# A softmax's maxima subtracted on TensorE under a second set of scores, in a four-layer attention stack

## The chip, the cores and the metric

The kernel runs on one core of one Trainium2 chip. The metric is the device time of one execution in microseconds (us). The engines are named as in the profile: PE is TensorE's matmul, PEld its weight load, DVE VectorE, ACT ScalarE, POOL GpSimd, SP the queue that issues DMAs.

## The reference

Input x has 16 sequences of 128 tokens with 256 features; a context of the same shape is given. Four layers follow one another, each with 16 heads of 16 features and a feed-forward part:

- the first attends over the heads inside each token (16 x 16 scores per token) and has a feed-forward of 1024;
- the second has two attentions, over x itself and over the context, in which the queries, keys, values and attention weights are rounded to steps of a given size (8 bits): `_fq(x) = (clip(round(x / delta) + zp, 0, 255) - zp) * delta`, and `softmax(_fq(q) @ _fq(k).T * 0.25)` is itself rounded to 8 bits with `zp` 0 before it meets the values; then a gated feed-forward;
- the third and fourth have two plain attentions each (softmax of q k / 4, some with masks) and a feed-forward.

Every softmax takes each row's maximum away before the exponential. In the second layer the scores, before their scale, are sums of products of integers.

## The kernel before

The 16 sequences go in 8 groups of two. `group` writes each group's work as steps; a step has a price per engine that may do it, the tiles it reads and writes, and a function that issues its instructions. All groups' steps go through one planner, `Plan.order`, which places them on the engines by prices, dependencies and free slots, and a shift per group and stage (`LEADS`); `least` is the earliest due time of a step. So the order on every engine is fixed when the kernel is built, and a change of any price moves steps everywhere. Every engine works its own queue strictly in that order. Where a step offers two engines, the planner picks one.

Memory: a large arena in SBUF, four PSUM banks `pw` for products and transposes, and one PSUM slot `ps` of four banks for scores (`SLOTS`, line 67). One set of scores for one sequence and 16 heads is 128 x 2048 fp32 and fills `ps`, so only one set is in flight at a time.

The second layer's attention is `quantized_attention` (line 1046) with `attention` (line 899): 8 groups x 2 attentions x 2 sequences = 32 batches. For a batch, `begin` (1091) issues the scores: eight bf16 matmuls of 32 rows, four strips of the array at once (`scores`, 832; line 844). Then `soft` does each half (8 heads, 128 x 1024) by itself: DVE takes the negated row maxima (1100), DVE adds them to the scores, out of PSUM into the arena (1113), ACT takes the exponential in place with the scale (1119), DVE sums the rows, inverts and scales the sums (1125 to 1128), POOL multiplies and rounds head by head (1134), ACT makes bf16 of it (1139). For 2 of the 64 halves the planner chose another way: ACT does eight exponentials with the maximum as bias and the row sum on the side (1104, 1106). A transposing DMA turns each half (913), and `products` (878, line 892) multiplies it with the values.

The third and fourth layers' attention is `plain_attention` (1199), 64 batches. It has the scores once in `ps` for the maxima (1243, or 1250 and 1255 under a mask), splits the negated maxima into three bf16 pieces whose sum is exact (1264 to 1272, DVE or POOL), transposes them on TensorE (1274), copies them to SBUF (1276), and then forms the scores a second time, transposed, with the maxima already added: 32 matmuls of 32 rows (1292), of which 16 are fp32 products of keys and queries and 16 are bf16 products that lay the maxima of one head over its block, with the constant 0/1 matrix `three_of` as weights. In that loop, for each of four heads of a strip, keys come first in the even ones and maxima in the odd ones. In the masked cross attention of layer three, `laid` (852, line 855) lays a mask under the scores in the same way, four bf16 matmuls of 512 columns.

Other lines that the prediction names: 686 and 699 are the fp32 products with weights (four matmuls, eight records in the trace, per step), 658 the transposes, 645 the loads of weights, 745 or 746 the addition or multiplication of a row (POOL or DVE), 732 or 733 the normalisation (ACT or DVE), 674 or 675 the scaling after a transpose, 1310 and 1313 the plain exponentials.

Of the kernel before, what the change touches and what calls it, by code (L numbers as in the profile page):

```python
# [8 lines left out]
F32 = mybir.dt.float32  # L9
BF16 = mybir.dt.bfloat16  # L10
I32 = mybir.dt.int32
U8 = mybir.dt.uint8
AF = mybir.ActivationFunctionType
ALU = mybir.AluOpType
AX = mybir.AxisListType

P = 128
B, S, D, H, DH, FF = 16, 128, 256, 16, 16, 1024
# [54 lines left out]


LEADS = [
    [79, -243, 396, 61, 306, 431, -218, 552, 246, -1043, 475, -1, 382, -725, -212, 120, 529, 352, 259, 257],
    [-1469, -506, -432, -870, -252, -175, -212, -889, -146, -178, -511, -754, -160, -374, -1202, -416, -1438, 67, -497, -72],
    [-408, -392, -516, 558, -136, 688, -438, -458, -1053, 58, -79, 304, 253, -385, -261, -277, -707, 386, 101, -525],
    [-618, -910, 247, -450, -186, 137, 135, 293, -265, -318, 61, -448, 441, -1039, -573, 1607, 326, 1399, 704, 1265],
    [118, 30, 704, -227, 45, 608, 400, 898, 1076, 334, 689, -396, 866, 605, -189, 715, 221, 931, 98, 676],  # L80
    [136, -318, -131, -829, 314, 611, -344, 561, 524, -90, 424, -258, 680, 156, 257, 416, 338, 931, 1112, 654],
    [117, 16, 354, -72, -34, 620, 249, 955, -58, -43, -427, 64, 340, 435, 246, 1312, 557, 1079, 605, 296],
    [586, 96, 831, 335, 623, 330, -23, 781, 930, 238, 205, 94, 1033, -120, -401, 948, 200, 1214, 848, 332],
]
CONTEXT = 18
HANDOVER = {"PE": 0.25, "-": 0.0}
# [65 lines left out]
class Plan:  # L152
# [3 lines left out]
    def block(self, kind, shape, dtype=F32, role=None):  # L156
        b = Block(kind, shape, dtype)
        if role is not None:
            sec = self.section
            b.section, b.role, b.turn = sec, role, sec.made[role]  # L160
            sec.made[role] += 1
            sec.units[role] = max(sec.units[role], b.units)
        return b
# [264 lines left out]
def decoder_stack_kernel(ctx: ExitStack, tc: tile.TileContext, a: dict, out: bass.AP):  # L428
# [97 lines left out]
    def small(n, *shape):  # L526
        return block("sm", [P, n] if not shape else [P, *shape])
# [4 lines left out]
    def prepare():  # L532
# [33 lines left out]

            G.tensor_scalar(m1, m1, -1.0e9, 1.0, ALU.mult, ALU.mult)

        step([("POOL", 5.0, masks)], reads=[raw, dl_token], writes=[mask_token], least=110.0)


        for dst, n, src, eye, dtype in ((m1T, S, m1, ident, F32), (kmT, B, km, ident[:B, :B], F32), (m3T, S, m3, ident, F32)):
# [287 lines left out]
    def paired(e):  # L860

        return e.rearrange("p (s i) k -> p s i k", i=2) if len(e.shape) == 3 else e.rearrange("p (s i) -> p s i", i=2)

    def wide(v):
        return paired(v).unsqueeze(3).to_broadcast([P, 4, 2, S])

    def values(dtype):


# [29 lines left out]
    def attention(x, wo, begin, soft, out_of, vz, dtype, after):  # L899


        plan.enter(after=after, w=1, oT=1, e=2, eT=2, **({"r": 1} if dtype == F32 else {"eb": 2}))
        wo = weight(wo)
        oT = block("m", [P, 2, NT], role="oT")
        for j in range(GB):
            ps, held = begin(j)
            eTs = []
            for c in range(2):
                e = soft(ps, j, c, held[c])
                eT = block("m", [P, 8, S], dtype, role="eT")  # L910
                eTs.append(eT)
                step(
                    [("SP", 1.2, lambda e=e, eT=eT: nc.sync.dma_start_transpose(out=eT.ap(), in_=e.ap().rearrange("p q k -> p (q k)")), None, 1.0)],
                    reads=[e], writes=[eT],
                )
            out_of(oT, eTs, vz, j)
        ps = psum()
        tokens_first(wo, oT, ps)
        add_to(x, ps)
# [126 lines left out]
    def quantized_attention(x, i, hT, kvT):  # L1046
# [44 lines left out]
        def begin(j):  # L1091
            tok = slice(j * S, (j + 1) * S)
            ps, issue = scores(None, lambda r, c: qT(r, c, tok), lambda r, c: kz(r, c, tok), True)
            es = [block("m", [P, 8, S], role="e") for _ in range(2)]
            step([("PE", 0.24, issue, "rows")], reads=[qk], writes=[ps], holds=es[:1])
            return ps, es

        def soft(ps, j, c, e):
            m, r, bias = small(8), small(8), small(8)
            step([("DVE", 1.22, lambda: V.tensor_reduce(paired(m.ap()), ps.ap()[:, :, c], AX.X, ALU.max, negate=True))], reads=[ps], writes=[m])  # L1100
            along = lambda: taken.eng == "ACT"

            def per_head():
                A.activation(bias.ap(), m.ap(), AF.Copy, scale=one(sc))
                for q in range(8):
                    A.activation(
                        e.ap()[:, q, :], ps.ap()[:, q // 2, c, q % 2], AF.Exp, bias=bias.ap()[:, q : q + 1], scale=one(sc),
                        accum_out=r.ap()[:, q : q + 1],
                    )

            taken = step(
                [
                    ("DVE", 1.22, lambda: V.tensor_tensor(paired(e.ap()), ps.ap()[:, :, c], wide(m.ap()), ALU.add), None, 2.6),  # L1113
                    ("ACT", 6.0, per_head, "exp"),
                ],
                reads=[ps, m], writes=[e, r, bias],
            )
            step(
                [("ACT", lambda: 0.0 if along() else 1.3, lambda: None if along() else A.activation(e.ap(), e.ap(), AF.Exp, scale=one(sc)), "exp")],  # L1119
                reads=[e], writes=[e],  # L1120
            )

            def inverse():
                if not along():
                    V.tensor_reduce(r.ap(), e.ap(), AX.X, ALU.add)  # L1125
                V.reciprocal(r.ap(), r.ap())

                V.tensor_scalar(r.ap(), r.ap(), delta(3), 0.0, ALU.mult, ALU.max)  # L1128

            step([("DVE", lambda: 0.5 if along() else 1.72, inverse)], reads=[e], writes=[r])  # L1130

            def share():
                for q in range(8):
                    G.tensor_scalar(e.ap()[:, q, :], e.ap()[:, q, :], r.ap()[:, q : q + 1], MAGIC, ALU.mult, ALU.add)  # L1134

            step([("POOL", 3.15, share)], reads=[e, r], writes=[e])
            eb = block("m", [P, 8, S], BF16, role="eb")

            step([("ACT", 1.05, lambda: A.activation(eb.ap(), e.ap(), AF.Relu, bias=top, scale=-1.0))], reads=[e], writes=[eb])  # L1139
            return eb  # L1140
# [4 lines left out]
            step([("ACT", 0.48, lambda: A.activation(oT.ap()[:, :, j * S : (j + 1) * S], po.ap(), AF.Copy, scale=one(dwv)))], reads=[po], writes=[(oT, j)])  # L1145

        attention(x, wo, begin, soft, out_of, vz, BF16, [*qk.writer.values()])

    def keys_and_values(kvT, wk, wv, biases, kz, vz):
        pk, pv = psum(), psum()  # L1150
# [48 lines left out]
    def plain_attention(x, qxT, kvT, ws, biases, mask=None, masked=None, cost=0.9, masked_T=None, key_mask=None, held=(), may_be_empty=False, there=None):  # L1199
# [29 lines left out]
        def batch(j):  # L1229
# [29 lines left out]
                if may_be_empty:  # L1259
                    step([("DVE", 0.18, with_key)], reads=[m], writes=[m])  # L1260

            def split(eng, m=m, rest=rest, mq=mq):
                piece = lambda n: mq.ap().rearrange("p (s r) -> p s r", r=32)[:, :, 0:12].rearrange("p s (f n) -> p s f n", n=3)[:, :, :, n]
                four = lambda t: t.ap().rearrange("p (s f) -> p s f", f=4)
                eng.tensor_copy(piece(0), four(m))  # L1267
                eng.tensor_tensor(four(rest), four(m), piece(0), ALU.subtract)
                eng.tensor_copy(piece(1), four(rest))
                eng.tensor_tensor(piece(2), four(rest), piece(1), ALU.subtract)  # L1270

            step([("DVE", 1.0, lambda split=split: split(V)), ("POOL", 1.25, lambda split=split: split(G))], reads=[m], writes=[rest, mq])
            pt, mt = block("pw", [P, S], BF16), block("m", [P, S], BF16, role="mt")
            step([("PE", 0.1, lambda pt=pt, mq=mq: T.transpose(pt.ap(), mq.ap(), ident_b))], reads=[mq], writes=[pt], holds=[mt])
            step(
                [("ACT", 0.32, lambda pt=pt, mt=mt: A.copy(mt.ap(), pt.ap())), ("DVE", 0.25, lambda pt=pt, mt=mt: V.tensor_copy(mt.ap(), pt.ap()))],
                reads=[pt], writes=[mt],
            )

            eTs = [block("m", [P, 8, S], role="eT") for _ in range(2)]  # L1280

# [2 lines left out]
            def issue(pT=pT, mt=mt, tok=tok):  # L1284
                if masked_T is not None:
                    laid(pT.ap(), *masked_T)
                for f in range(4):
                    c, i = divmod(f, 2)
                    for part in (0, 1) if i else (1, 0):
                        for s in range(4):  # L1290
                            r = strip(s)
                            T.matmul(  # L1292
                                pT.ap()[:, s, c, i], lhsT=kz.ap()[r, c, i, tok] if part else three_of[r, f, :],
                                rhs=qT.ap()[r, c, tok] if part else mt.ap()[r],
                                start=masked_T is None and part == 1 - i, stop=(f == 3 or masked_T is None) and part == i,
                            )

            step(
# [181 lines left out]
```

## Time and profile before

| what | value |
|---|---|
| median of 3 runs | 1440.99 us |
| lowest, highest | 1439.8, 1448.02 us |
| profiled execution, its own time | 1440.68 us |
| its span, first to last instruction | 1438.9 us |
| mean granted TensorE clock | 0.98 |

A group's row in the profile reads: line, engine, operation, out<-in by tile name, shapes, count | busy time, mean ns of one | idle time of the engine just before, and what ended it. A timeline row reads: start us, length us, engine, line, operation, tiles, shape, count. The matmul records of four strips overlap, so the time that a group costs TensorE is read from its start to the next group's start. The slices are 40 equal parts of the span, about 36 us each.

### The profile page before, as it was taken

What the parts mean: (1) busy time and instruction counts of PE and PEld (TensorE: products, weight loads), DVE (VectorE), ACT (ScalarE), POOL (GpSimd) and SP (SyncE); (2) the same over time, 40 slices, a digit from 0 to 9 for tenths busy, and PEclk for the clock granted to TensorE, in tenths of its full rate; (3) what the DMA queues carried; (4) which work ended last, traced back from release to release, by engine and by line L of the source; (5) the groups of instructions that cost most, each with busy time, mean ns of one, the idle gap of its engine ahead of it and who ended that gap; (6) DMA issues with size and microseconds to landing.
All of it is one profiled execution on the core that took longest, in us unless ns stands there. A gap on an engine that the chain in (4) does not pass through costs nothing.

```text
span 1438.9 us, 36661 instructions
## 1 busy us (share of the span) xinstructions
PE 1358.0 (94%) x15219; PEld 1116.4 (78%) x15219; DVE 1042.8 (72%) x1608; ACT 837.6 (58%) x1480; POOL 596.8 (41%) x1393
## 2 busy tenths in 40 slices
PE   8899969986989999898998999999999999999998
PEld 7778857875868888687786888888887887878887
DVE  1663597888897578959788777867786867685961
ACT  4662568876675766646547656646553545366442
POOL 2022575847777236615515453434122425141201
PEclk9999989998999999999999999999999999999999
DMA  7466434442432326422221431200022111000000
GB/s 231 104 187 203 167 81 126 129 110 56 111 74 58 90 50 176 115 90 77 74 68 45 108 96 28 89 16 17 2 92 71 39 64 31 32 2 2 9 17 22
DMA packets 192646, 113.67 MB, mean 79 GB/s; under 512 B 139088, under 2 KB 181728, under 8 KB 192352
## 3 DMA queue, kind: packets, MB, share of 16 engines
q1 hardware_dynamic: 192480, 111.33, 28.3%
q8 instruction: 119, 1.95, 0.5%
q14 instruction: 47, 0.39, 0.1%
HBM read 67.26 MB, written 27.26 MB: 66 GB/s over the span
## 4 chain that ended last, share of the span: by engine, by line
PE 79%; DVE 9%; ACT 2%; issue 1%; POOL 1%; DMA 1%; SPq 0%; DVEq 0%; ACTq 0%; POOLq 0%
PE pw L699 27%; PE pw L686 27%; PE pw L892 9%; PE ps L1292 6%; PE ps L844 5%; PE pw L658 3%; DVE arena L1113 2%; DVE sm L1100 2%; DVE sm L1125 1%; DVE arena L962 1%; DVE sm L1243 1%; PE pw L987 1%; DVE arena L1250 1%; DVE sm L1255 1%; DVE sm L715 0%
## 5 line engine op out<-in xcount | busy, mean ns | idle before, releaser
L686 PE MATMUL pw<-arena 128*128 128x256 f32 x2048 | 486.9, 388 | 10.6 <-ACT arena L674 8.2
L699 PE MATMUL pw<-arena 128*128 128x256 f32 x2048 | 481.1, 386 | 2.1 <-ACT arena L665 1.6
L686 PEld LDWEIGHTS pw<-arena 128*128 128x128 f32 x2048 | 383.3, 193 | 80.4 <-issue 11.3
L699 PEld LDWEIGHTS pw<-arena 128*128 128x128 f32 x2048 | 382.6, 192 | 64.1 <-issue 9.2
L1134 POOL TENSOR_SCALAR arena<-arena,sm 128x128 f32<-128x128 f32 x512 | 186.7, 386 | 106.1 <-DVE sm L1128 71.9
L1325 DVE RECIPROCAL arena<-pw 128x256 f32<-128x256 f32 x64 | 112.1, 1752 | 90.1 <-PE pw L892 77.2
L745 POOL TENSOR_TENSOR arena<-arena,rows 128x512 f32<-128x512 f32 x109 | 139.4, 1281 | 84.7 <-ACT arena L732 72.2
L812 ACT ACTIVATE arena<-pw,cols_sb 128x256 f32<-128x256 f32 x188 | 80.0, 471 | 77.7 <-PE pw L686 70.9
L707 DVE TENSOR_TENSOR arena<-pw,arena 128x512 f32<-128x512 f32 x88 | 59.9, 682 | 77.4 <-PE pw L699 76.9
L732 ACT ACTIVATE arena<-arena,sm,sm 128x256 f32<-128x256 f32 x151 | 83.8, 595 | 31.8 <-POOL sm L725 30.7
L1292 PE MATMUL ps<-arena 32*128 32x128 f32 x2048 | 97.4, 299 | 3.3 <-DVE sm L1243 2.5
L1139 ACT ACTIVATE arena<-arena,top 128x1024 bf16<-128x1024 f32 x64 | 73.4, 1147 | 41.4 <-POOL arena L1134 35.5
L892 PE MATMUL pw<-arena 128*32 128x128 f32 (+1 forms) x2560 | 88.5, 266 | 9.1 <-DMA arena<-arena 5.3
L844 PE MATMUL ps<-arena 32*128 32x256 f32 (+1 forms) x1280 | 84.7, 371 | 12.0 <-DVE arena L1113 11.4
L658 PE MATMUL pw<-ident,arena 128*128 128x128 f32 x416 | 69.0, 292 | 27.1 <-ACT arena L732 19.3
L1292 PEld LDWEIGHTS ps<-arena 32*128 32x128 f32 x2048 | 75.8, 188 | 23.0 <-issue 10.4
L721 POOL TENSOR_SCALAR sm<-sm 128x2 f32<-128x2 f32 x88 | 17.2, 195 | 183.7 <-DVE sm L716 179.5
L1267 POOL CAST mq<-sm 128x16 bf16<-128x16 f32 x50 | 11.1, 222 | 196.1 <-DVE sm L1243 107.6
L1310 ACT ACTIVATE arena<-arena 128x1024 f32<-128x1024 f32 x64 | 66.5, 1054 | 41.5 <-DVE arena L1306 40.5
L872 POOL MEMSET arena<- 128x512 f32 (+1 forms) x48 | 25.0, 526 | 155.4 <-PE pw L699 56.9
L1119 ACT ACTIVATE arena<-arena,sc 128x1024 f32<-128x1024 f32 x62 | 70.6, 1147 | 31.3 <-DVE arena L1113 31.2
L1250 DVE TENSOR_TENSOR arena<-ps,m 128x1024 f32<-128x1024 f32 x64 | 78.0, 1219 | 12.4 <-PE ps L844 8.0
(141 smaller groups left out, 2069.4 us busy)
## 6 DMA issues: line engine op xcount, KB each, us to landing
mha<-arena SPq DMA_DIRECT2D x16, 512.0 KB, 4.5
ca<-arena SPq DMA_DIRECT2D x16, 512.0 KB, 4.2
arena<-mha SPq DMA_DIRECT2D x16, 512.0 KB, 5.2
arena<-ca SPq DMA_DIRECT2D x16, 512.0 KB, 3.9
arena<-in_L_xattn_ff_w_dram SPq DMA_DIRECT2D x29, 256.0 KB, 3.0
dqkv<-arena SPq DMA_DIRECT2D x8, 768.0 KB, 4.0
arena<-dqkv SPq DMA_DIRECT2D x16, 384.0 KB, 4.0
arena<-in_L_xattn_ffn_w_dram SPq DMA_DIRECT2D x18, 256.0 KB, 3.2
```

What stands on the lines that cost most here:

```text
L658: T.transpose(p[:, c, j * S : (j + 1) * S], s[:, j, c * P : (c + 1) * P], ident)
L686: T.matmul(ps.ap()[:, m, :], lhsT=w.ap()[:, k, m * P : (m + 1) * P], rhs=t.ap()[:, k, :], start=(k == 0), stop=(k == 1),)
L699: T.matmul(ps.ap()[:, j, :], lhsT=lhs(k, j) if lhs else t.ap()[:, k, j * S : (j + 1) * S], rhs=w.ap()[:, k, :], start=start and j + k == 0 ...
L732: ("ACT", 0.6, lambda j=j: A.activation(xh.ap()[:, j, :], x.ap()[:, j, :], AF.Identity, bias=nb.ap()[:, j : j + 1], scale=rstd.ap()[:, j : ...
L745: ("POOL", 1.33, lambda: G.tensor_tensor(dst.ap(), src.ap(), row(name), op)),
L812: "ACT", 0.47, lambda ps=ps, h=h, m=m, bias=bias: A.activation(h.ap()[:, m, :], ps.ap()[:, m, :], func, bias=bias),
L844: T.matmul(ps.ap()[:, s, c] if i is None else ps.ap()[:, s, c, i], lhsT=left(r, c) if i is None else left(r, c, i), rhs=right(r, c), start ...
L892: T.matmul(po.ap()[32 * s : 32 * s + 32, 2 * ones + c, :], lhsT=lhsT, rhs=n255 if n else eTs[c].ap()[:, 2 * s + i, :], start=i == n == 0, ...
L1134: G.tensor_scalar(e.ap()[:, q, :], e.ap()[:, q, :], r.ap()[:, q : q + 1], MAGIC, ALU.mult, ALU.add)
L1250: [("DVE", 1.22, lambda e=e, c=c: V.tensor_tensor(paired(e.ap()), ps.ap()[:, :, c], mask[0].unsqueeze(1).unsqueeze(1).to_broadcast([P, 4, ...
L1292: T.matmul(pT.ap()[:, s, c, i], lhsT=kz.ap()[r, c, i, tok] if part else three_of[r, f, :], rhs=qT.ap()[r, c, tok] if part else mt.ap()[r], ...
L1325: step([("DVE", 1.75, lambda po=po, r=r: V.reciprocal(r.ap(), po.ap()[:, 2:4, :]))], reads=[po], writes=[r])
```

## The change

Four things are changed.

1. In `quantized_attention`, `begin` now issues the scores, takes all 16 heads' negated maxima in one DVE instruction, splits, transposes and copies them by the helper `turned_maxima` (taken out of `plain_attention`, unchanged), and issues the scores a second time into `ps`, under which four bf16 matmuls of 512 columns lay the maxima. `soft` takes the exponential on ACT straight out of PSUM; the subtraction on DVE and the way with eight exponentials are gone. The attention's section holds one more small tile (`mt=1`).
2. In `plain_attention`, the loop of the 32 transposed matmuls issues all 16 laid ones first and then the 16 of keys and queries.
3. The step that makes `three_of` has its due time at 75 in place of 110.
4. The table `LEADS` has other numbers, so that the order on every engine is another one.

```diff
-        plan.enter(after=after, w=1, oT=1, e=2, eT=2, ...)
+        plan.enter(after=after, w=1, oT=1, mt=1, e=2, eT=2, ...)
...
-            step([("PE", 0.24, issue, "rows")], reads=[qk], writes=[ps], holds=es[:1])
+            step([("PE", 0.24, issue, "rows")], reads=[qk], writes=[ps])
+            m, rest, mq = small(16), small(16), block("mq", [P, P], BF16)
+            step(
+                [("DVE", 2.3, lambda ps=ps: V.tensor_reduce(m.ap(), ps.ap().rearrange("p s c i k -> p (s c i) k"), AX.X, ALU.max, negate=True))],
+                reads=[ps], writes=[m],
+            )
+            mt = turned_maxima(m, rest, mq)
+
+            def less(ps):
+                for s in range(4):
+                    T.matmul(
+                        ps[:, s].rearrange("p c i k -> p (c i k)"), lhsT=mt.ap()[strip(s)],
+                        rhs=three_of[strip(s)].rearrange("p f k -> p (f k)"), start=True, stop=False,
+                    )
+
+            ps, issue = scores(less, lambda r, c: qT(r, c, tok), lambda r, c: kz(r, c, tok), True)
+            step([("PE", 0.46, issue, "rows")], reads=[qk, mt, mask_token], writes=[ps], holds=es[:1])
...
-            step([("DVE", 1.22, lambda: V.tensor_reduce(paired(m.ap()), ps.ap()[:, :, c], AX.X, ALU.max, negate=True))], reads=[ps], writes=[m])
...
-                    ("DVE", 1.22, lambda: V.tensor_tensor(paired(e.ap()), ps.ap()[:, :, c], wide(m.ap()), ALU.add), None, 2.6),
-                    ("ACT", 6.0, per_head, "exp"),
...
+                [("ACT", 1.15, lambda: A.activation(paired(e.ap()), ps.ap()[:, :, c], AF.Exp, scale=one(sc)), "exp")],
+                reads=[ps], writes=[e],
...
+    def turned_maxima(m, rest, mq):
+        def split(eng):
+            piece = lambda n: mq.ap().rearrange("p (s r) -> p s r", r=32)[:, :, 0:12].rearrange("p s (f n) -> p s f n", n=3)[:, :, :, n]
+            four = lambda t: t.ap().rearrange("p (s f) -> p s f", f=4)
+            eng.tensor_copy(piece(0), four(m))
+            eng.tensor_tensor(four(rest), four(m), piece(0), ALU.subtract)
+            eng.tensor_copy(piece(1), four(rest))
+            eng.tensor_tensor(piece(2), four(rest), piece(1), ALU.subtract)
+        step([("DVE", 1.0, lambda: split(V)), ("POOL", 1.25, lambda: split(G))], reads=[m], writes=[rest, mq])
+        pt, mt = block("pw", [P, S], BF16), block("m", [P, S], BF16, role="mt")
+        step([("PE", 0.1, lambda: T.transpose(pt.ap(), mq.ap(), ident_b))], reads=[mq], writes=[pt], holds=[mt])
+        step(
+            [("ACT", 0.32, lambda: A.copy(mt.ap(), pt.ap())), ("DVE", 0.25, lambda: V.tensor_copy(mt.ap(), pt.ap()))],
+            reads=[pt], writes=[mt],
+        )
+        return mt
...
-                for f in range(4):
-                    c, i = divmod(f, 2)
-                    for part in (0, 1) if i else (1, 0):
+                for part in range(2):
+                    for f in range(4):
+                        c, i = divmod(f, 2)
                         for s in range(4):
...
-                                start=masked_T is None and part == 1 - i, stop=(f == 3 or masked_T is None) and part == i,
+                                start=masked_T is None and part == f == 0, stop=part == 1 and f == 3,
```

## The prediction

> **What bounds the kernel now.** I read the page's busy shares first, then its slices of time, then a table of busy time by stretch, and last the groups and the timeline of the lines that the change touches.
>
> ```profile
> PE 1358.0 (94%) x15219; PEld 1116.4 (78%) x15219; DVE 1042.8 (72%) x1608; ACT 837.6 (58%) x1480; POOL 596.8 (41%) x1393
> ...
> PE   8899969986989999898998999999999999999998
> ...
> DVE  1663597888897578959788777867786867685961
> ...
> PEclk9999989998999999999999999999999999999999
> ```
>
> TensorE is busy 94% of the span and nearly without a hole in its second half; in slices 6 to 12 (180 to 432 us) it has holes, VectorE stands at 7 to 9 tenths, and the clock is lower. By stretch (length, then PE, PEld, DVE, ACT, POOL busy, then clock, DMA share, GB/s):
>
> ```profile
> 0.00:180.00 180.00, 165.74 (x1291) 139.15 (x1295) 86.74 (x226) 95.12 (x218) 50.27 (x105) 0.99 0.61 178
> 180.00:460.00 280.00, 240.18 (x2208) 196.32 (x2201) 240.69 (x401) 201.10 (x336) 195.55 (x461) 0.93 0.39 92
> 460.00:560.00 100.00, 99.54 (x901) 83.23 (x903) 69.13 (x117) 67.97 (x120) 40.19 (x91) 1.00 0.35 91
> 560.00:700.00 140.00, 130.56 (x1640) 105.22 (x1633) 109.41 (x149) 82.53 (x147) 70.81 (x164) 0.98 0.39 109
> 700.00:840.00 140.00, 130.06 (x1545) 105.42 (x1545) 117.35 (x170) 82.57 (x131) 61.00 (x144) 0.98 0.29 76
> 840.00:1000.00 160.00, 159.81 (x1969) 131.78 (x1967) 114.12 (x162) 92.11 (x150) 63.55 (x151) 1.00 0.15 41
> 1000.00:1439.00 439.00, 432.07 (x5687) 355.27 (x5685) 305.34 (x389) 216.22 (x384) 115.40 (x281) 1.00 0.10 33
> ```
>
> This table carries the forecast. Where VectorE is busy 69 to 71% (460 to 560, 840 to 1000, 1000 to 1439), TensorE is busy 98 to 100% at clock 1.00. Where VectorE is at 78 to 84% (560 to 840), TensorE loses 7%. Where it is at 86% (180 to 460), TensorE loses 14% and the clock falls to 0.93. The quantized attentions fill just these stretches. Losses: 39.8 us idle and 280 x 0.07 = 19.6 us of clock in 180 to 460, together 59; 9.4 + 9.9 = 19.4 idle and 280 x 0.02 = 5.6 of clock in 560 to 840, together 25. So 84 us are open to a lighter VectorE. The rest of the span is TensorE's own work, and there each added matmul counts in full.
>
> ```profile
> L1100 DVE TENSOR_REDUCE sm<-ps 128x8 f32<-128x1024 f32 x64 | 77.8, 1215 | 8.5 <-PE ps L844 8.4
> ...
> L1113 DVE TENSOR_TENSOR arena<-ps,sm 128x1024 f32<-128x1024 f32 x62 | 75.8, 1222 | 3.5 <-ACT arena L1156 0.5 <-ACT arena L1119 0.2
> ...
> L1243 DVE TENSOR_REDUCE sm<-ps 128x16 f32<-128x2048 f32 x32 | 73.0, 2281 | 11.4 <-PE ps L844 11.4
> ...
> L1119 ACT ACTIVATE arena<-arena,sc 128x1024 f32<-128x1024 f32 x62 | 70.6, 1147 | 31.3 <-DVE arena L1113 31.2
> ```
>
> L1113 is the subtraction that goes. L1243 is the twin of the new reduction: the same 16 x 128 scores in one instruction.
>
> **The change part by part.**
>
> *VectorE.* Out: 62 subtractions, 75.8 us, and 64 reductions of 1.215, 77.8 us. In: 32 reductions of 2.281, 73.0 us. The splits of 32 more batches go mostly to POOL: in the changed instruction order 84 of 96 lie there (50 of 64 before), so VectorE has 12 against 14. The planner also gives VectorE 9 more row additions (0.825 each), 8 more normalisations (0.41) and 7 more scalings (0.53), 14 us. Net: about -67 us. 35 of the 62 subtractions lie in 180 to 460, and 36 of the 64 reductions: there -42.8 - 43.7 + 18 x 2.281 = -45, and VectorE comes to about 195 of 280, 70%.
>
> *TensorE, second scores.* The prices are distances between starts of neighbouring groups:
>
> ```profile
> 403.57 0.40 PE L844 MATMUL ps<-arena 32*128 32x256 bf16 x8
> 403.89 0.66 PE L658 MATMUL pw<-ident,arena 128*128 128x128 f32 x4
> ...
> 425.05 0.23 PE L1274 MATMUL pw<-ident_b,mq 128*128 128x128 bf16 x1
> 425.12 1.95 PE L686 MATMUL pw<-arena 128*128 128x256 f32 x8
> ...
> 437.53 0.50 PE L1292 MATMUL ps<-arena 32*128 32x128 f32 x8
> 437.85 0.29 PE L1292 MATMUL ps<-arena,three_of 32*128 32x128 bf16 x8
> 437.96 0.68 PE L1292 MATMUL ps<-arena 32*128 32x128 f32 x16
> ```
>
> and, from a later piece of the timeline,
>
> ```profile
> 502.49 0.39 PE L855 MATMUL ps<-arena,three 32*128 32x512 bf16 x4
> 502.72 1.03 PE L844 MATMUL ps<-arena 32*128 32x256 f32 x16
> ```
>
> Eight score matmuls take 0.32, the four laid ones in front of them 0.23 (same shape and type as L855's), the transpose of the maxima 0.07: 0.62 x 32 = 20 us. A product step of eight records takes 1.73 in long runs (13.83 for 64) and about 0.1 more before another shape; since the new groups often stand beside other small ones I take one such step per batch, 3 us (bounds 0 and 2 x 0.1 x 32 = 6). Together +23. All of it lies on TensorE's queue, which sets the end; nothing hides it except holes that remain.
>
> *TensorE, order in the transposed scores.* The same 32 matmuls, 64 times. The first eight fp32 records take 0.32 where sixteen in the middle take 0.50 (437.96 to the next group's start at 438.46), so a change from fp32 to bf16 inside the step costs about 0.07; the new order has one such change fewer inside. 64 x 0.07 = -4.5 us. No row shows the new order; bounds: -0.14 x 64 = -9 (both inner changes cost that) and +0.1 x 64 = +6 (sixteen short ones in a row run worse). I take -4.5, the nearest row. The first matmul now needs the turned maxima where the fp32 ones did not; that is 0.3 us of head start lost when the maxima are late, inside those bounds.
>
> *The new chain and the slot.* All scores share one slot `ps`. Before, a batch held it 0.4 + 0.3 (L1100's wait behind the first scores in the timeline) + 4 x 1.22 = 5.6 us. Now twice: 0.4 + 0.3 + 2.28 = 3.0, and 0.55 + 0.3 + two exponentials of about 1.1 (L1313 from PSUM: 1.03 and 1.11; from the arena 1.15) = 3.1. Between them the slot is free, while split (four POOL operations of 0.23), transpose and copy (0.26) run, some 4.4 us from scores to second scores. In the changed order 31 of the 32 second scores stand 6 to 90 us of TensorE work behind their first ones, one 1.2 us. So the wait is covered, except once (3 us); if POOL's shares (eight of 0.37, 3 us) stand in front of a split, up to 7.5 us are needed, which the 6 to 8 us cases just cover. The second scores are queued in front of products that need neither, so a late split stops them all; the exponential now waits for TensorE where it waited for L1113.
>
> *ACT, POOL, SP.* ACT: the same exponentials, 29 more copies of 0.26, six more table loads of 1.28, minus the 16 per-head exponentials of 0.67: +5 us at 58%. POOL: 34 more splits of 0.92, 9 row additions of 1.28 fewer: +20 us; in 180 to 460 about 212 of 280, 76%. SP: 150 weight loads for 126, since planned evictions differ; with 126 no product waited for one by more than 0.2 us, the cover being loads issued ahead (3 us to landing); if all 24 were late, 72 us. I take 0. The LEADS and the earlier mask step only set the order.
>
> *What the lighter VectorE returns.* Bounds: 0 and 84 us. By the table's stretches at 70% all of the loss in 180 to 460 would go; but POOL at 76% and ACT at 72% stay, every batch's chain is longer, and L658's wait for ACT's normalised rows (19.3 us in all) is no wait for VectorE. I take half of 59, 30, and 10 of the 25 behind it: -40.
>
> The Trainium skill, "TensorE: Matmul & The Clock Gate", section "What's actually happening", has the clock fall to half after an idle window of about 3.4 us and return after as much work, 1.7 us lost each time. With six waits that long (TensorE's longest are 7.1, 5.0, 4.9 and 4.5 us) that is an estimate of 10 us of clock to win, where the row's 0.93 says 19.6; by the rule my sum would end some 5 us higher. The trace agrees that idleness is what lowers it: the stretches without holes show 1.00.
>
> **Sum.** +23 - 4.5 - 40 = -21.5. The profiled execution took 1440.7 us (span 1438.9), the median is 1441.0, so 0.3 is to be added at most: 1419 us.
>
> **Rivals.**
> *(a) TensorE's added work wins (slower).* The holes in 180 to 460 come from the long chain (share, transposing DMA, product: the page's wait of TensorE for L1113 is only 11.4 us in four pieces) and not from VectorE's load; then they stay, and +23 - 4.5 stands alone: 1459. For it: few of TensorE's waits name VectorE directly. Against: the table, in which the holes follow VectorE's share. It decides below 18.5 us of returned loss.
> *(b) A draw.* POOL takes VectorE's place in the dense stretches, as it gets the splits in front of its shares: at 76% it lies between the 71% without holes and the 78% with 7%, 0.05 x 280 = 14 us idle and as much clock; 59 - 28 = 31 returned in the first stretch, nothing in the second, and late splits, one in three of the 32 by 1 us, take 10 back: 18.5 - 21 = -2.5, 1438.
> *(c) Everything returns.* The 180 to 460 stretch looks like 460 to 560: -84 + 18.5, 1375. Against: POOL and ACT load there.
> *(d) The reordered transposed scores do not gain.* +6 for -4.5: 1430.
> *(e) The slot is the limit in the dense stretch.* Every batch holds it 6.1 us for 5.6: 32 x 0.5 = 16 more, 1435. Against: TensorE's wait for the slot's reader L1113 is 11.4 us in all. The Trainium skill, "TensorEngine Tiling (Array Packing)", section "PSUM Bottleneck", warns of this: packed matmuls speed up TensorE, not the emptying of PSUM. By that rule (e) would be the likeliest; the row of waits does not bear it out.
>
> **How the numbers follow.** About 1% (14 us) is what a measurement tells from no change; the runs lie 8 us apart. Chances: my forecast with (c) and (d) 0.60 (0.44, 0.06, 0.10), (b) 0.20, (e) 0.05, (a) 0.15. (d) ends 0.75% below, so half of it counts as the same. Faster by over 1%: 0.44 + 0.06 + 0.05 = 0.55; within 1%: 0.30; slower: 0.15. Range: from 1395 (two thirds of the 84 returned and the favourable ends of the rest: 20 - 9 - 56 = -45) to 1453 ((a) with its favourable ends, 20 - 9 = +11, 1452); left out are (c) and most of (a), under 0.2. The likeliest's own range is 1405 to 1432 (-40 give or take a third).
>
> **What would show it.** Right: L1113's group gone; VectorE near 975 us; in the dense stretch clock over 0.95, and TensorE's idle time (81 us) under 60; TensorE's busy time above 1358 or nearly so in a shorter span; the transposed step under 1.4 us from first to last start. Wrong: idle time as before with waits of the laid matmuls for the copied maxima, or of products for weights; then (a). If the second scores cost more than 0.8 us each, or the transposed step grows, the sum's first two terms fail.

## The result

The changed kernel takes 1434.8 us (median of 6 runs, 1432.1 to 1436.2) and the kernel before 1443.1 (6 runs, 1439.8 to 1448.0): ratio 0.9939, 95% interval 0.9919 to 0.9960. It is faster by 0.6%, 8.3 us, where 21.5 were forecast. The profiled execution took 1435.07 us, its span is 1433.3, 5.6 below that of before.

From the page of the changed kernel, busy time and slices:

```profile
PE 1371.6 (96%) x15635; PEld 1115.6 (78%) x15635; DVE 983.3 (69%) x1537; ACT 832.7 (58%) x1466; POOL 622.9 (43%) x1520
...
PE   8888999889999999799999999999999999999898
...
DVE  1762578787587677858947679578567767769671
...
PEclk9999999999999999899999999999999999999999
```

TensorE's busy time is up by 13.6 us in a span shorter by 5.6, so its idle time went from 80.9 to 61.7. VectorE has 59 us less. The holes of slices 6 to 12 are mostly gone, but slices 3 and 4 show 8 where 9 stood, and slice 17 shows 7 where 8 stood. By stretch, with the columns as before:

```profile
0.00:180.00 180.00, 160.62 (x1215) 134.45 (x1216) 87.61 (x213) 96.46 (x210) 58.98 (x136) 0.97 0.62 179
180.00:460.00 280.00, 264.57 (x2474) 211.26 (x2472) 212.67 (x387) 204.64 (x354) 196.68 (x475) 0.97 0.40 91
460.00:560.00 100.00, 98.97 (x1139) 81.47 (x1142) 69.23 (x107) 54.40 (x105) 38.94 (x85) 1.00 0.37 111
560.00:700.00 140.00, 129.65 (x1615) 102.11 (x1611) 108.49 (x167) 90.73 (x148) 79.60 (x208) 0.95 0.37 99
700.00:840.00 140.00, 138.88 (x1599) 112.68 (x1591) 96.06 (x140) 82.08 (x133) 60.97 (x153) 1.00 0.35 96
840.00:1000.00 160.00, 155.84 (x2102) 126.10 (x2101) 121.84 (x167) 95.52 (x157) 76.67 (x189) 1.00 0.29 79
1000.00:1433.00 433.00, 423.11 (x5511) 347.59 (x5509) 287.39 (x363) 208.83 (x363) 111.08 (x277) 0.99 0.08 26
```

Counted as in the prediction (idle time plus length times missing clock): 180 to 460 lost 59.4 us and now loses 15.4 + 8.4 = 23.8; 560 to 840 lost 25 and loses 11.5 + 7.0 = 18.5. That is 42 us returned where the forecast looked. But 0 to 180 lost 16.1 and now loses 19.4 + 5.4 = 24.8, and what follows 840 lost 7.1 and now loses 4.2 + 9.9 + 4.3 = 18.4. With 0.6 in 460 to 560, 21 of the 42 us are given back outside the stretches.

This count takes some time twice: idle time that falls into a stretch of half clock is in both of its terms. The trace keeps the clock as windows of whole or half clock. Summed over the windows of half clock of the whole kernel (length, then busy times as above), in the kernel before (first) and in the changed one (second):

```profile
sum 58.03, PE 38.02 PEld 27.55 DVE 51.95 ACT 37.10 POOL 44.53; mean PE 4.75 PEld 3.44 DVE 6.49 ACT 4.64 POOL 5.57
sum 47.78, PE 39.74 PEld 29.38 DVE 31.12 ACT 22.67 POOL 30.34; mean PE 4.42 PEld 3.26 DVE 3.46 ACT 2.52 POOL 3.37
```

TensorE works in 38.0 of the 58.0 us. Work at half clock takes twice its time (a product step 3.46 us for 1.73, shown at the end), so half clock cost it 19.0 us and not 29; in the changed kernel it cost 19.9. Idle time plus this loss, by the same stretches: 180 to 460 lost 51.6 and now loses 22.4; 560 to 840 lost 24.9 and now loses 17.3, so 37 us came back; 0 to 180, 460 to 560 and the rest from 840 on lost 16.0, 0.5 and 7.0 and now lose 23.4, 1.0 and 17.3, so 18 went again. Half of the gain in the stretches stays, 18 to 19 us. This second count is used from here on.

What TensorE waited for in the changed kernel (us in total, times, longest):

```profile
PE ps L1102 <- ACT arena L1312: 7.6, 2, 4.0
...
PE pw L658 <- DVE rows L626: 4.6, 1, 4.6
PE pw L686 <- ACT arena L674: 4.6, 6, 1.3
...
PE ps L1102 <- DVE sm L1095: 2.4, 2, 1.9
...
PE pw L1157 <- POOL mq L1153: 0.9, 2, 0.7
```

L1102 are the laid matmuls of the second scores. They wait 7.6 us for a plain attention's exponential that still reads the slot, and 2.4 for a reduction; TensorE's wait for splits on POOL is 0.9 us in all. No wait of a product for its weights is among those over 0.2 us.

The prices, first the second scores in the changed kernel's timeline then the transposed step:

```profile
228.69 0.40 PE L1102 MATMUL ps<-three_of,arena 32*128 32x512 bf16 x4
228.92 0.39 PE L844 MATMUL ps<-arena 32*128 32x256 bf16 x8
229.24 0.23 PE L1157 MATMUL pw<-ident_b,mq 128*128 128x128 bf16 x1
229.31 1.95 PE L699 MATMUL pw<-arena 128*128 128x256 f32 x8
```

0.23 + 0.32 + 0.07 = 0.62 us a batch, as forecast; in the other batches at whole clock and without a wait the first two take the same 0.55. The transposed step is shown in the first experiment, whose order is that of the kernel before.

### The profile page after: what moved, and what is told of

It is laid out like the page before. It is cut to its first block, busy times and chain, and to the rows that moved or that the text cites. A ratio compares the mean times of both kernels' runs of the same rounds, so it can differ in the third digit from the quotient of the medians.

```text
span 1433.3 us, 37574 instructions
## 1 busy us (share of the span) xinstructions
PE 1371.6 (96%) x15635; PEld 1115.6 (78%) x15635; DVE 983.3 (69%) x1537; ACT 832.7 (58%) x1466; POOL 622.9 (43%) x1520
## 4 chain that ended last, share of the span: by engine, by line
PE 54%; DVE 1%; ACT 1%; DMA 0%; issue 0%; ACTq 0%; DVEq 0%
PE pw L686 19%; PE pw L699 17%; PE pw L889 8%; PE ps L1291 5%; PE ps L844 4%; PE pw L658 1%; PE pw L1157 0%; DMA arena<-arena 0%; DVE sm L1258 0%; PE ps L855 0%; DVE arena L1324 0%; PE ps L1102 0%; ACT arena L674 0%; DVE arena L1265 0%; ACT arena L1312 0%
## 5 line engine op out<-in xcount | busy, mean ns | idle before, releaser
L745 POOL TENSOR_TENSOR arena<-arena,rows 128x512 f32<-128x512 f32 x100 | 128.5, 1286 | 81.3 <-ACT arena L732 68.7
L1150 POOL CAST mq<-sm 128x16 bf16<-128x16 f32 x84 | 19.1, 227 | 315.1 <-DVE sm L1258 107.4
L812 ACT ACTIVATE arena<-pw,cols_sb 128x256 f32<-128x256 f32 x186 | 78.4, 472 | 81.9 <-PE pw L686 73.8
L732 ACT ACTIVATE arena<-arena,sm,sm 128x256 f32<-128x256 f32 x143 | 79.5, 595 | 42.7 <-POOL sm L725 39.3
L844 PE MATMUL ps<-arena 32*128 32x256 f32 (+1 forms) x1536 | 98.4, 357 | 5.7 <-DVE sm L1258 2.9
L1119 DVE TENSOR_REDUCE sm<-arena 128x8 f32<-128x1024 f32 x64 | 77.6, 1212 | 21.7 <-ACT arena L1114 20.5
L674 ACT ACTIVATE arena<-pw,cols_sb 128x256 f32<-128x256 f32 x131 | 67.6, 563 | 39.8 <-PE pw L658 39.5
L1159 ACT COPY arena<-pw 128x128 bf16<-128x128 bf16 x93 | 24.2, 263 | 106.7 <-PE pw L1157 106.0
L1258 DVE TENSOR_REDUCE sm<-ps 128x16 f32<-128x2048 f32 x32 | 73.0, 2282 | 14.2 <-PE ps L844 13.8
L658 PE MATMUL pw<-ident,arena 128*128 128x128 f32 x416 | 65.9, 288 | 16.0 <-DMA arena<-in_x_dram 5.2
```

What stands on the lines that cost most here:

```text
L658: T.transpose(p[:, c, j * S : (j + 1) * S], s[:, j, c * P : (c + 1) * P], ident)
L732: ("ACT", 0.6, lambda j=j: A.activation(xh.ap()[:, j, :], x.ap()[:, j, :], AF.Identity, bias=nb.ap()[:, j : j + 1], scale=rstd.ap()[:, j : ...
L745: ("POOL", 1.33, lambda: G.tensor_tensor(dst.ap(), src.ap(), row(name), op)),
L812: "ACT", 0.47, lambda ps=ps, h=h, m=m, bias=bias: A.activation(h.ap()[:, m, :], ps.ap()[:, m, :], func, bias=bias),
L844: T.matmul(ps.ap()[:, s, c] if i is None else ps.ap()[:, s, c, i], lhsT=left(r, c) if i is None else left(r, c, i), rhs=right(r, c), start ...
```

## The experiments

The theory on record: the lighter VectorE returns TensorE's holes (-40), the second scores cost 23, the order in the transposed step brings 4.5. The rival that the result suggests: the whole gain is the transposed step's, and the second scores repay just what they cost. A second rival: the holes belong to the planned order, not to any engine's load.

### The order in the transposed step alone

The kernel before with part 2 of the change (the start and stop flags that go with it are left out here):

```diff
-                for f in range(4):
-                    c, i = divmod(f, 2)
-                    for part in (0, 1) if i else (1, 0):
+                for part in range(2):
+                    for f in range(4):
+                        c, i = divmod(f, 2)
```

> The kernel before with part 2 alone: in the transposed scores of the plain attentions all 16 laid matmuls come first; prices and LEADS are untouched, so the order of steps is the one before. In the trace of the changed kernel the 48 records of such a step take 1.28 us from start to next start, 1.43 before. If the 0.15 us lie on TensorE's path 64 times, the time falls by 9.6 us, about 1433.5. The forecast on record took 4.5 us (1438.5). If the step is hidden in waits, no change.

Measured: 1433.28 us, ratio 0.9940 (0.9927 to 0.9952), -9.3 us. The timeline of this kernel, same step as the one of the prediction at 437.53:

```profile
437.49 0.40 PE L1292 MATMUL ps<-arena,three_of 32*128 32x128 bf16 x16
437.72 1.11 PE L1292 MATMUL ps<-arena 32*128 32x128 f32 x32
438.77 0.23 PE L1274 MATMUL pw<-ident_b,mq 128*128 128x128 bf16 x1
```

437.49 to 438.77 is 1.28 us where 437.53 to 438.96 was 1.43. The 16 laid matmuls take 0.23 together, as before (0.11 + 0.11); the 32 fp32 records take 1.05 where 0.32 + 0.50 + 0.39 = 1.21 stood. The old order changes twice from fp32 to bf16 inside the step, behind the first eight and behind the middle sixteen; the new one does not. At the new order's 1.05 for 32 and the same last group, the two changes come to 0.16 together. 0.15 x 64 = 9.6 us, all of it on the path. This one loop, of the same instructions, is as much as the whole change. That the change of type is what costs is the reading that fits these rows; the new order also has one change from bf16 to fp32 fewer and another order of accumulation, which no run separates.

### The second scores alone

The changed kernel with the old loop in the transposed step (the diff above, reversed).

> The changed kernel with the old loop in the transposed scores. If the whole gain of the change comes from that loop, this is back at the time before or slightly above, 1443 to 1446. If the second scores and the lighter VectorE bring a gain of their own, as the forecast has it (+23 - 40), it stays at least 5 us below the kernel before.

Measured: 1443.39 us, ratio 1.0008 (0.9999 to 1.0017). Parts 1, 3 and 4 together change nothing that can be measured. The account against the kernel before, from the page of this kernel (first) and its windows of half clock summed (second); its span is 1441.1 us:

```profile
PE 1377.8 (96%) x15635; PEld 1123.2 (78%) x15635; DVE 984.9 (68%) x1537; ACT 833.4 (58%) x1466; POOL 621.9 (43%) x1520
```

```profile
sum 44.35, PE 36.01 PEld 26.34 DVE 28.21 ACT 24.18 POOL 30.38; mean PE 4.50 PEld 3.29 DVE 3.53 ACT 3.02 POOL 3.80
```

Idle: 1441.1 - 1377.8 = 63.3 for 80.9, so 17.6 returned; half clock: 36.0 / 2 = 18.0 for 19.0, so 1.0 returned; together 18.6. The span is 2.2 longer, so TensorE's own work grew by 21 us: 20 are the 0.62 of each batch, and about 1 goes with the additional changes of shape around them. The median is only 0.9 us above that of before, so each of these sums is good to a microsecond or two.

### What a lighter VectorE returns when the order stays

The kernel before, with the row sums over 16 of 128 keys:

```diff
-                    V.tensor_reduce(r.ap(), e.ap(), AX.X, ALU.add)
+                    V.tensor_reduce(r.ap(), e.ap()[:, :, 0:16], AX.X, ALU.add)
```

> The kernel before, in its order, with the row sums of the quantized attention taken over 16 of the 128 keys (this leaves out most of the sum): 62 instructions of 1.21 us become about 0.3, so that VectorE loses some 57 us, as much as by the change, and no engine gains work. If TensorE's holes follow VectorE's load, as the forecast's table was read, 25 to 40 us return: 1403 to 1418. If the holes are set by the fixed order and the length of each batch's chain, under 12 us return, above 1430.

The kernel leaves out most of the sum. Measured: 1436.78 us, ratio 0.9960 (0.9949 to 0.9972), -6 us. VectorE's busy time fell by 51 us to 992, nearly as far as the change takes it. The dense stretch of this kernel:

```profile
180.00:460.00 280.00, 242.21 (x2213) 197.72 (x2206) 215.19 (x401) 201.38 (x338) 196.23 (x462) 0.93 0.38 92
```

VectorE is at 77% where it was at 86, and TensorE's idle time is 37.8 us for 39.8, at the same clock of 0.93. So in this order VectorE's share as such does not make TensorE's holes, though they stand in the same stretches. Two things are not shown by it. The forecast was for a new order, made with the lighter VectorE; and it is the sums that were shortened, not the subtraction, which the change removes and on which TensorE's waits of 11.4 us end. A kernel with the subtraction cut to one of eight heads has no measured time.

### A shorter chain, and both together

The eight share operations of a half on POOL become one:

```diff
-                for q in range(8):
-                    G.tensor_scalar(e.ap()[:, q, :], e.ap()[:, q, :], r.ap()[:, q : q + 1], MAGIC, ALU.mult, ALU.add)
+                G.tensor_scalar(e.ap(), e.ap(), r.ap()[:, 0:1], MAGIC, ALU.mult, ALU.add)
```

> The kernel before, in its order, with the eight share operations of a half on POOL replaced by one over all eight heads with the first head's factor (this leaves out the other heads' factors). POOL loses an estimated 1.5 us per half, some 90 of 187 us, and each batch's chain from scores to products is about 3 us shorter. If the holes of the fixed order are the latency of that chain, 10 us or more return; if the order holds work back wherever it was planned, under 6 us, as with the short sums.

> Both at once: one share operation per half on POOL and the row sums over 16 keys on VectorE (leaves out the other heads' factors and most of the sums), order as before. If VectorE and the chain together make the holes, most of the 59 us of the stretch 180 to 460 us return and the time is under 1410. If the holes belong to the order, the two savings add up to some 12 us or less, above 1428.

The first kernel leaves out the other heads' factors, the second also most of the sums. Measured: one share 1440.52 us, ratio 0.9990 (0.9981 to 1.0000); both 1439.68, ratio 0.9978 (0.9967 to 0.9989). POOL went from 597 to 483 us (one operation of 1.13 us for eight of 0.37), VectorE to 989, and the time by at most 3 us; the two savings do not even add up to the 6 of the short sums alone. In the stretch 180 to 460 of the kernel with both:

```profile
180.00:460.00 280.00, 240.96 (x2176) 196.81 (x2176) 213.12 (x400) 199.49 (x334) 130.12 (x208) 0.92 0.39 92
```

VectorE is at 76%, POOL at 46%, and TensorE's 39 us of holes are all there. One of them, in the timeline of the kernel before and of this one:

```profile
200.20 0.30 PE L892 MATMUL pw<-arena 128*32 128x128 bf16 x4 [5.03 <-DMA arena<-arena]
```

```profile
199.36 0.30 PE L892 MATMUL pw<-arena 128*32 128x128 bf16 x4 [5.05 <-DMA arena<-arena]
```

The products that wait for the transposing DMA wait as long, whatever POOL and VectorE have saved by then. The trace shows why at this place: the share on POOL ended at 194.71 and 191.34 us, but the conversion to bf16 that follows it began at 195.93 and 195.06. In ACT's queue it stands behind two scalings, which wait for a product of TensorE, and behind another half's exponential, all back to back. So neither the sums nor the shares make this hole, and taking work off them returns next to nothing in this order. The other holes were not traced one by one.

### More work on VectorE

The changed kernel with the row sums taken twice:

```diff
                 V.tensor_reduce(r.ap(), e.ap(), AX.X, ALU.add)
+                V.tensor_reduce(r.ap(), e.ap(), AX.X, ALU.add)
```

> The changed kernel, in its order, with the row sums of the quantized attention taken twice: 64 instructions of 1.21 us more, 78 us, which puts VectorE above where it stood before the change. If VectorE's load makes the holes, 25 to 40 us are lost: 1460 to 1475. If not, under 12 us.

Measured: 1472.89 us, ratio 1.0215 (1.0197 to 1.0234), against the changed kernel's 0.9939: +38 us, with VectorE's busy time up by 72 us to 1055. The waits of TensorE in this kernel (line numbers behind the edit are one higher than in the changed kernel):

```profile
PE ps L844 <- DVE sm L1095: 10.9, 4, 7.6
PE ps L1102 <- ACT arena L1313: 9.0, 2, 5.4
PE ps L844 <- DVE sm L1259: 6.9, 2, 3.9
```

Reductions and exponentials that held the slot for 2.1, 7.6 and 2.9 us too long hold it for 10.9, 9.0 and 6.9. These three make 14 of the 34 us by which TensorE's idle time grows (96.0 for 61.7). So a fixed order looks one-sided: work that the plan did not expect is paid for by half here, and work that is taken out returned a ninth (6 of 51) above. The two figures come from two kernels with different orders.

### The second scores without their score matmuls

```diff
-            ps, issue = scores(less, lambda r, c: qT(r, c, tok), lambda r, c: kz(r, c, tok), True)
+            ps = block("ps", [P, 4, 2, 2, S])
+            issue = lambda ps=ps: less(ps.ap())
```

> The changed kernel with the eight score matmuls of the second set left out (the laid maxima alone go to the exponential), 256 matmuls fewer, order of steps kept. If all of the second scores' time lies on TensorE's path, as the forecast took it, 32 x 0.32 = 10 us less: 1424.5. If half of it stands in holes, 5 us or less.

The laid matmuls then also end their sums. The kernel leaves out the eight score matmuls that go over the laid maxima. Measured: 1428.59 us, ratio 0.9903 (0.9891 to 0.9916), 6.2 us below the changed kernel. The 10 us that were expected count 0.32 for the removed group. But part of that is the change to the next group's tile shape, and it does not go:

```profile
227.98 0.40 PE L1102 MATMUL ps<-three_of,arena 32*128 32x512 bf16 x4
228.31 0.23 PE L1158 MATMUL pw<-ident_b,mq 128*128 128x128 bf16 x1
```

The laid group now takes 0.33 to the next start and not 0.23, so 0.22 a batch are gone, 7.0 us in all; the span is 6.9 shorter, with TensorE's idle time at 62.2 for 61.7. TensorE's work is paid in full. This also speaks against the added matmuls having merely filled holes.

### The two tables of LEADS exchanged

> The changed kernel with the LEADS of the kernel before. If the shifts only set an order that matters little, within 5 us of 1434.8. If the planned order is a term of its own, slower by 10 us or more, with new holes on TensorE that no removed or added work explains.

> The kernel before with the LEADS of the changed kernel. The changed kernel with the old LEADS took 1628 us. If each table fits only the steps that it was made for, this is slower by 50 us or more; if the new table is the better one for any steps, it is at or below 1443.

Measured: the changed kernel with the old LEADS 1628.26 us, ratio 1.1288 (1.1271 to 1.1306); the kernel before with the new ones 1576.29, ratio 1.0926 (1.0904 to 1.0947). The slices of the first:

```profile
PE   8899989889788989899899978999899989966557
...
PEclk9999989999989889999999988999899999977678
```

The loss is in holes all along and in a tail in which TensorE is half busy at a clock of 0.6 to 0.8: what was left at the end had nothing beside it. A table fits the steps that it was made for. A table of the wrong steps costs 130 to 190 us, more than any other term here. That is no measure of how far two tables made for the same steps lie apart; the next experiment has that.

### The order made anew

LEADS were moved at random and kept when the planned order got shorter by the planner's own prices; no instruction is added or taken out.

```diff
-                [("PE", 1.15 if masked_T is None else 2.1, issue, "rows")],
+                [("PE", 1.3 if masked_T is None else 2.1, issue, "rows")],
```

The price is changed in the first of three kernels; the other two keep 1.15 and had a shorter search.

> The kernel before with the laid matmuls first, the planner's price for that step put at 1.3 in place of 1.15, and LEADS moved by a random search until the planned order no longer got shorter. No instruction is added or taken out. If the order is a term of its own that can be bettered, below 1428; if the old LEADS were as good as they get, 1430 to 1440.

> The same with the old price of 1.15 and LEADS moved from the old ones by a shorter search. Below 1430 if the order can be bettered; 1430 to 1440 if not.

> The changed kernel with its LEADS moved by the same search. If the second scores give the planner room that the kernel before lacks, this is at least 4 us below the best of the two without them; if the second scores only repay their cost, within 4 us of it or above.

Measured, in this order: 1426.43 us, ratio 0.9882 (0.9859 to 0.9905); 1433.04, 0.9931 (0.9907 to 0.9954); 1432.07, 0.9923 (0.9897 to 0.9950). The first is the best kernel of the study, without second scores: 1.2% below the kernel before and 8 us below the changed one. Its dense stretch:

```profile
180.00:460.00 280.00, 252.78 (x2256) 205.38 (x2255) 243.18 (x418) 199.91 (x333) 187.09 (x434) 0.96 0.39 89
```

VectorE is at 87%, no less than in the kernel before, and TensorE's idle time in the stretch is 27.2 us for 39.8. So the holes there can be closed in part without touching VectorE. But they moved more than they went: TensorE's idle time over the whole span is 78.5 us, and 79.7 in the kernel with the transposed step alone (1430.6 - 1350.9). With the loss by half clock, 17.1 for 21.8, the new order returns 6 us of the whole, which fits the span's 5.0.

The same count over the kernels with tables made for them shows a line between them: without second scores TensorE loses 96 to 102 us in idle time and by half clock, the best replanned one included; with them 78 to 82. So in the orders tried the second scores come with some 18 us less loss, and with about as much work (21 us).

The second and third kernels, with the same search, end within a microsecond of each other. The searches were of different length and one for each, so that they do not show that the second scores can not gain with a better order; that stays open.

## Why the prediction was wrong

The sign was right; the size was not, -8.3 for -21.5. The sign was luck as far as the main idea goes: second scores and lighter VectorE together come to no change, and the gain is the small loop's. That the time falls on rival (e)'s 1435 is a coincidence too, since its cause, the slot, is not found. By the steps of the prediction:

- *VectorE's net saving, 67 us*: 59 measured. A small miss.
- *Second scores, +23*: +21. The 0.62 a batch was right; the changes of shape around the new groups cost about 1 us and not 3, inside the bounds given for them.
- *Order in the transposed step, -4.5*: the term was mis-sized, -9.3. The old order has two inner changes from fp32 to bf16, behind the first eight records and behind the middle sixteen, and the new order has none; I counted one fewer. The 0.50 for the sixteen that I compared with had such a change in it. The bound, -9, had both.
- *The chain and the slot*: right. Splits on POOL cost TensorE 0.9 us and those on DVE as much, and its wait for slot readers ahead of L1102 is 7.6 + 2.4 + 1.8 us. Rival (e), and the Trainium skill's "PSUM Bottleneck" in "TensorEngine Tiling (Array Packing)" behind it, found no more support here than that.
- *ACT, POOL, SP*: ACT -5 for +5, POOL +26 for +20; 150 loads of weights for 126 and no product late for them. Nothing hangs on these. Rival (b) had POOL at 76% of the dense stretch; it is at 70.
- *What the lighter VectorE returns, -40*: this is the step that failed. In the stretches that it named 37 us came back, so there its size was nearly right. But it put the rest of the span at nothing, "TensorE's own work", and there 18 were lost: in the first 180 us and from 840 us on, in the new order. 18 to 19 remain. Its upper bound of 84 us was too wide as well, 76.5 without the time counted twice. Its reason is not shown: in the order before, a relief of VectorE by sums returned 6 us, and with POOL's relief added 3. The table showed where the load and the holes stand together. That was a correlation, and I priced it as a cause.
- *"The LEADS and the earlier mask step only set the order"*: the order is no side matter. Exchanging the tables costs 9 and 13%, and three orders of the kernel with the transposed step changed take 1433.3, 1433.0 and 1426.4 us. A forecast of a change that makes every queue anew has to carry the order's own spread.

Of the signs that were named ahead, L1113's group is gone, VectorE stands at 983 us, the clock in the dense stretch at 0.97 and the transposed step at 1.28 us; TensorE's idle time, 61.7, just misses its 60.

With the measured sizes the sum reads +21 - 9.3 - 19 = -7, and the measured change is -8.3. The first and the third term come from one kernel, where together they must give the change of its span, +2.2; so this sum tests the middle term alone.

What is not settled: whether the 19 us came back because the plan could count on a lighter VectorE or because its LEADS were searched for longer. The doubled sums show that this order has little room for more work on VectorE (+38 us for 72). The best search without second scores got back 6 of the whole, so that no run here shows as much to be had without them; but none separates the two either.

On the clock: in the kernel before, TensorE idles 4.46 us ahead of a group of eight bf16 score matmuls, which then takes 0.61 us and not 0.40, and a step of eight product records behind it takes twice its 1.73.

```profile
409.01 0.61 PE L844 MATMUL ps<-arena 32*128 32x256 bf16 x8 [4.46 <-DVE arena L1113]
...
412.06 3.46 PE L686 MATMUL pw<-arena 128*128 128x256 f32 x8
```

This fits the halved clock after an idle window that the Trainium skill describes ("TensorE: Matmul & The Clock Gate", "What's actually happening"). The trace does not show one long wait behind every window of half clock: those at 53.4 and 609.8 us follow waits of 2.96 and 2.37 us. The estimate of 10 us that I drew from six long waits was low for the whole kernel, where half clock cost 19.0 us. The row's 19.6 for 180 to 460 was too high, with 11.8 of work lost there. In the changed kernel it is 7.0 in that stretch, but 19.9 in all, so half clock moved and did not go.

## What to carry to other kernels

Where every queue's order is planned, an engine that looks loaded beside another's holes is a suspicion, not a cause: shorten its instructions with the order kept, and see whether the holes move, before pricing its relief. Price what the new order may lose outside the stretches that you look at. Count a lowered clock on the work done under it alone; idle time is counted already. Then split a change into its parts; here the loop that seemed the smaller part was the whole gain, and the large part a draw. Group matmuls of one type where the order is free: in this step that was worth 0.15 us, 9 us in all.

## What the runs showed of the hardware that was not expected

- The same 32 matmuls of 32 rows (48 records) take 1.43 us with two inner changes from fp32 to bf16 and 1.28 without; the changes from bf16 to fp32 cost nothing that shows (0.11 us for eight of 32x128, at either place).
- Four bf16 matmuls of 32x512 take 0.23 us to the next start when a group of the same tile shape follows and 0.33 when one of 128*128 does.
- One POOL operation over 128 x 1024 takes 1.13 us, eight over 128 x 128 take 8 x 0.37 = 3.0.
